# Spreading the work-ahead pieces of a rotor attention over twice as many steps between the experts

## The chip, the cores and the metric

One NeuronCore of a Trainium2 chip runs the whole program; the others are idle. The metric is device time in microseconds (us) from launch to end of one execution; the median of several runs is given. The engines are PE (matrix multiply, results to PSUM), DVE (vector), ACT (scalar and table functions), POOL (general vector work without access to PSUM) and SP (issues DMAs). Each engine works off its own instructions in the order in which they were written.

## The reference

Two transformer layers on x of shape (16, 256, 128), all in float32. Layer 0 is a 16-head attention and a mixture of 16 experts (the best 4 of each token, computed here for all experts and weighted with zeros). Layer 1 is a "rotor" attention and a gated feed-forward part. The change touches the expert part and the piece of layer 1's attention that runs beside it:

```python
# layer 0, experts
gu = jnp.einsum('th,ehf->tef', x, gate_up_proj) + gate_up_bias
gate = jnp.minimum(gu[..., ::2], LIMIT)
up = jnp.clip(gu[..., 1::2], -LIMIT, LIMIT)
act = (up + 1.0) * gate * jax.nn.sigmoid(gate * ALPHA)
out = jnp.einsum('te,teh->th', scores, jnp.einsum('tei,eih->teh', act, down_proj) + down_bias)
...
# layer 1, attention
k = jnp.exp(1j * (k_real * PHASE_SCALE))
rotors = jnp.exp(1j * (t[:, None, None] * freqs))[None]
out_pos = holo(v, rotors, jnp.conj(rotors))        # real(cumsum(v * binder) * probe) / sqrt(t)
out_assoc = holo(v, jnp.conj(k_shifted), k)
out = (out_pos * g_pos + out_assoc * g_assoc).reshape(Bb, Tt, HD) @ Wo
```

A "piece" below is one of eight products of this kind for one block of 128 of the 1024 columns: position or association (`pos`, `assoc`), batch element k of two, cosine or sine s. Each takes a product with the binder, a running sum along time, a product with probe and gate, and an addition to a total.

## The kernel before

The batch is cut into eight chunks of two elements (512 tokens). The program has three stages: layer 0's attention, the experts, and layer 1.

The expert stage is a loop over 128 steps (`n`, lines 1044 to 1082): step n is expert e = n % 16 of chunk c = n // 16. Each step issues PE's matmuls of gate and up into PSUM (`gate_up`, line 759), their evacuation (DVE `g`, line 767; ACT `u`, line 769; ACT's Silu, line 772; POOL's clip, line 773), for the step before, DVE's product (line 779) and POOL's product with the routing weight (line 780) (`act`), and the down matmul of three steps before (`down`, line 783). `pg` has three PSUM buffers and `pup` two. The engines' order is the order of writing (`manual_schedule`), so where a piece of other work is written within a step is where it stands in every queue.

Other work is laid between these steps: 

- The chunk before is ended at e = 2 (`chunk_end1`); at e = 3 `into_stream` (line 800) transposes it on PE into the one-buffer PSUM pool `p_m` and DVE adds it to `x`; at e = 5 `figures` takes mean and variance, at e = 7 POOL's `normalizer` follows, and the next chunk's routing weights are transposed (`spread_scores`).
- `prepare` (line 813) is a generator called once a step: layer 1's modulation, the rotor angles (`angles`), scaled weights, and last `first_steps` (line 942), the first two projections of layer 1 with their sines and binders.
- `part_ahead` (line 876), also called once a step, computes for one chunk the last of the eight column blocks of layer 1's attention (j = 7) and keeps the sum in `totals`. It starts at e = 10 of the next chunk (e = 8 in the last): normalized tokens, transposes, projections `pv` and `pk`, `off` (ACT rounds, then DVE subtracts), sines and cosines, and the eight pieces: POOL `bind`, DVE `read` (a scan, a product, an addition) one step later. In every chunk but the last one piece a step; in the last two.
- `last_end` (line 1018) ends the last chunk's layer-0 attention and works off its routing on DVE, up to about chunk 2.

`p_m` has one buffer, so each user of it waits until the one before is read out. `past_others` (line 937) lets `first_steps` stay clear of steps that use it. `turn_rotor` (line 990) turns a block of angles into cosines and sines on ACT: blocks 7 and 6 in `prepare`, the others in the sine step of `part_ahead`.

The third stage (from line 1085) runs 57 steps of layer 1, with two long scans a step on DVE, three products on POOL and ten or more matmuls on PE.

Of the kernel before, what the change touches and what calls it, by code (L numbers as in the profile page):

```python
# [11 lines left out]
F32 = mybir.dt.float32  # L12
AF = mybir.ActivationFunctionType
ALU = mybir.AluOpType
# [4 lines left out]
P = 128  # L19
B, T, D = 16, 256, 128  # L20
NIT = T // P
NCH = B // 2
# [12 lines left out]
NE, TOPK = 16, 4  # L35
# [19 lines left out]
def tile_adaln_two_layers(ctx: ExitStack, tc: tile.TileContext, a: dict, out: bass.AP):  # L55
    nc = tc.nc
# [23 lines left out]
    half_pi = const.tile([P, 1], F32, tag="half_pi", name="half_pi")  # L80
# [47 lines left out]
    gates = const.tile([P, NJ, 2], F32, tag="gates", name="gates")  # L128
# [98 lines left out]
    with ExitStack() as moe_scope:  # L227
# [64 lines left out]
        cross = moe_scope.enter_context(tc.tile_pool(name="cross", bufs=2))  # L292
# [21 lines left out]
        with ExitStack() as scope:  # L314
# [5 lines left out]
            p_m = scope.enter_context(tc.tile_pool(name="pa_m", bufs=8, space=bass.MemoryType.PSUM))  # L320
# [368 lines left out]
            for n in range(len(rounds) + LAG + 1):  # L689
                if n < len(rounds):  # L690
# [4 lines left out]
                    s = scores(n)  # L695
# [41 lines left out]
        w_k1 = load_late("w_k1", [P, HD], a["Wk"])  # L737
# [4 lines left out]
        with ExitStack() as scope:  # L742
# [12 lines left out]
            keep_all, row = sums[:, 0, 0:1].to_broadcast([P, T]), sums[:, 1, :]  # L755
# [57 lines left out]
            def prepare():  # L813
# [62 lines left out]
            def part_ahead(c):  # L876


                j = NJ - 1
                tokens(c)  # L880
                yield
                yield
                into_tokens(c, turned(c, hns.pop(c), p_m, "a1"))
                yield
                flat = hTs[c].rearrange("p k t -> p (k t)")
                v = cross.tile([P, 2, T], F32, tag="o", name=f"v_ahead_{c}")
                pv = p_m.tile([P, 2, T], F32, tag="m", name=f"pv0_{c}")
                nc.tensor.matmul(pv, w_v1[:, ts(j, P)], flat, start=True, stop=True)
                nc.scalar.copy(v, pv)
                bound = {}  # L890

                def bind(nm, k, s, by):
                    t = cross.tile([P, T], F32, tag=("heads", "y")[s], name=f"bound_ahead_{nm}_{c}_{k}_{s}")
                    nc.gpsimd.tensor_tensor(t, v[:, k, :], by, ALU.mult)
                    bound[nm, k, s] = t

                def read(nm, k, s, i, probe):
                    dst = totals[c][:, k, :]
                    nc.vector.tensor_tensor_scan(row, keep_all, bound.pop((nm, k, s)), 0.0, ALU.mult, ALU.add)  # L899
                    first = i == 0 and s == 0  # L900
                    nc.vector.scalar_tensor_tensor(
                        dst if first else row, row, gates[:, j, i : i + 1], probe, ALU.mult, ALU.mult
                    )
                    if not first:
                        nc.vector.tensor_tensor(dst, row, dst, ALU.add)
# [3 lines left out]
                pieces = [  # L909
                    ("pos", k, s, 0, rotor[:, j, s, :], rotor[:, j, s, :]) for k in range(2) for s in range(2)  # L910
                ] + [("assoc", k, s, 1, cs[:, s, k, 0:T], cs[:, s, k, 1:]) for k in range(2) for s in range(2)]
                many = 2 if c == AHEAD - 1 else 1

                def go(i):
                    for q in pieces[max(i - 1, 0) * many : i * many]:
                        read(*q[:4], q[5])
                    for q in pieces[i * many : (i + 1) * many]:
                        bind(*q[:3], q[4])

                for i in range(8 // many + 1):  # L920
                    yield
                    if i == 0:
                        pk = p_m.tile([P, 2, T], F32, tag="m", name=f"pk0_{c}")
                        nc.tensor.matmul(pk, w_k1[:, ts(j, P)], flat, start=True, stop=True)
                        off = cross.tile([P, 2, T], F32, tag="hn4", name=f"off_ahead_{c}")
                        nc.scalar.activation(off, pk, AF.Copy, bias=ROUND)
                        nc.vector.scalar_tensor_tensor(off, off, ROUND, pk, ALU.subtract, ALU.subtract)
                    if i == 1:
                        nc.scalar.activation(cs[:, 1, :, 1:], off, AF.Sin, scale=-TWO_PI_IN)
                        nc.scalar.activation(off, off, AF.Abs)  # L930
                        nc.scalar.activation(cs[:, 0, :, 1:], off, AF.Sin, bias=half_pi, scale=-TWO_PI_IN)

                        for r in {2: (0,), 3: (1,), 4: (2,), 5: (3,), 6: (4, 5)}.get(c, ()):
                            turn_rotor(r)
                    go(i)

            def past_others():

                while at["step"] % NE in (3, 7):
                    yield  # L940

            def first_steps():

                flat = hTs[0].rearrange("p k t -> p (k t)")
                for n in range(2):
# [6 lines left out]
                    nc.scalar.copy(v, pv)  # L952
                    firsts[n] = {"v": v}
                    yield
                    yield from past_others()
# [4 lines left out]
                    off = whole  # L960
                    nc.vector.scalar_tensor_tensor(off, whole, ROUND, pk, ALU.subtract, ALU.subtract)
                    cs = phasor[n]
                    yield
# [23 lines left out]
                hTs[c] = hT2[c]  # L987
                modulated(c, pt, 0, 1, [hTs[c][:, k, :] for k in range(2)])

            def turn_rotor(j):  # L990

                cos, sin = rotor[:, j, 0, :], rotor[:, j, 1, :]
                nc.scalar.activation(cos, sin, AF.Abs)
                nc.scalar.activation(cos, cos, AF.Sin, bias=half_pi, scale=-1.0)
                nc.scalar.activation(sin, sin, AF.Sin)

            both = [P, 2, 2, T]
            firsts = {}
# [44 lines left out]
            at, ahead = {}, []  # L1043
            for n in range(total + 4):
# [508 lines left out]
```

## Time and profile before

| | us |
|---|---|
| median of three runs | 1106.1 (1105.72 to 1106.27) |
| the profiled execution | 1105.43 |
| its span, first to last instruction | 1103.6 |
| expert stage, first gate matmul | 302.6 |
| expert stage, last down matmul's end | 702.4 |

In the profile each engine's busy time is given as a share of the span; "idle before" is the time in which an engine had nothing running before an instruction, with the instruction whose end released it. The costliest groups that belong to the expert stage are these; columns are line, engine, operation, out<-in with shapes and count, then busy us and mean ns of one, then idle us before them and what ended most of it:

```profile
L780 POOL TENSOR_TENSOR u<-u,wide 128x512 f32<-128x512 f32 x128 | 164.0, 1281 | 37.0 <-DVE u L779 29.2
L788 PE MATMUL acc<-u,w_dn 128*128 128x512 f32 x256 | 133.4, 603 | 9.8 <-POOL u L780 9.7
L763 PE MATMUL pg<-hT,w_gu 128*128 128x512 f32 x256 | 133.0, 601 | 8.3 <-DVE u L779 7.8
L765 PE MATMUL pup<-hT,w_gu 128*128 128x512 f32 x256 | 130.8, 592 | 0.0
L767 DVE TENSOR_SCALAR g<-pg,b_gu 128x512 f32<-128x512 f32 x128 | 95.4, 745 | 41.0 <-PE pg L763 39.8
L779 DVE SCALAR_TENSOR_TENSOR u<-u,pg 128x512 f32<-128x512 f32 x128 | 86.9, 679 | 24.4 <-POOL u L773 23.3
```

Each matmul of 512 columns is two instructions, whose ends the profile models; successive starts are closer than the mean length.

### The profile page before, as it was taken

To read this page: it belongs to the slowest core of one execution; us is meant where nothing else is said; L and a number is where in the kernel's file an instruction comes from. 1 tells how busy PE (TensorE), PEld (TensorE's weight loads), DVE (VectorE), ACT (ScalarE), POOL (GpSimd) and SP (SyncE) were. 2 spreads that over 40 slices of the span, in tenths; PEclk is the share of its full clock that TensorE was granted. 3 is DMA by queue.
4 is the path that set the end of the run, shared out by engine and by line. 5 is a ranking of instruction groups with operands and counts; after the bars stand their busy time and mean duration, and the time that the engine had idled before them with its cause. 6 is when DMAs were issued, how large, how long until landed. Compare 5 with 4: busy or idle time off the path is not lost.

```text
span 1103.6 us, 16066 instructions
## 1 busy us (share of the span) xinstructions
PE 1028.1 (93%) x5319; PEld 516.5 (47%) x5319; DVE 911.4 (83%) x1417; ACT 689.5 (62%) x1391; POOL 803.6 (73%) x762
## 2 busy tenths in 40 slices
PE   7999999999999999999899999797999999999987
PEld 5566666666644444444344444233343443434333
DVE  6678878998565886978486877998999999999994
ACT  3676667666656465566666465464666657667573
POOL 3335443552567677777679877799999999999992
PEclk9999999999999999999999999899999999999999
DMA  3102100000142222222222222000000000000000
GB/s 115 41 15 65 51 2 3 3 4 2 63 148 79 80 94 97 77 96 79 77 78 96 81 92 76 1 0 1 1 0 10 0 11 10 1 10 1 10 6 24
DMA packets 31955, 46.80 MB, mean 42 GB/s; under 512 B 8032, under 2 KB 22784, under 8 KB 31872
## 3 DMA queue, kind: packets, MB, share of 16 engines
q1 hardware_dynamic: 31328, 45.51, 12.3%
q8 instruction: 42, 0.69, 0.2%
q14 instruction: 41, 0.34, 0.1%
q10 hardware_dynamic: 544, 0.26, 0.1%
HBM read 43.13 MB, written 2.37 MB: 41 GB/s over the span
## 4 chain that ended last, share of the span: by engine, by line
PE 49%; DVE 28%; ACT 9%; POOL 6%; issue 6%; DMA 1%; SPq 0%; DVEq 0%; ACTq 0%; POOLq 0%
DVE sum_assoc L1153 6%; DVE mem L1153 6%; PE acc L788 5%; PE pg L763 5%; PE s L403 5%; PE pup L765 5%; PE st L437 5%; PE po L457 5%; PE pout L1167 4%; DVE m_pos L1384 4%; POOL u L780 2%; DVE sums L899 2%; DVE u L779 2%; PE pq L530 2%; DVE g L767 1%
## 5 line engine op out<-in xcount | busy, mean ns | idle before, releaser
L780 POOL TENSOR_TENSOR u<-u,wide 128x512 f32<-128x512 f32 x128 | 164.0, 1281 | 37.0 <-DVE u L779 29.2
L445 ACT ACTIVATE exp<-st 128x512 f32<-128x512 f32 x256 | 132.2, 602 | 85.9 <-PE st L437 85.9
L415 DVE TENSOR_REDUCE maxima<-s 128x2 f32<-128x512 f32 x256 | 158.9, 684 | 26.3 <-PE s L403 26.0
L1167 PE MATMUL pout<-m_pos,w_pos 128*128 128x512 f32 x228 | 114.8, 627 | 30.8 <-DVE m_pos L1384 20.8
L788 PE MATMUL acc<-u,w_dn 128*128 128x512 f32 x256 | 133.4, 603 | 9.8 <-POOL u L780 9.7
L763 PE MATMUL pg<-hT,w_gu 128*128 128x512 f32 x256 | 133.0, 601 | 8.3 <-DVE u L779 7.8
L769 ACT ACTIVATE u<-pup,b_gu 128x512 f32<-128x512 f32 x128 | 87.0, 680 | 74.3 <-PE pup L765 69.4
L1153 DVE TENSOR_TENSOR_SCAN sum_assoc<-keep,bound_assoc 128x1024 f32<-128x1024 bf16 x57 | 129.9, 2279 | 2.0 <-POOL bound_assoc L1150 1.9
L765 PE MATMUL pup<-hT,w_gu 128*128 128x512 f32 x256 | 130.8, 592 | 0.0
L1153 DVE TENSOR_TENSOR_SCAN mem<-keep,bound_pos 128x1024 f32<-128x1024 bf16 x57 | 129.5, 2272 | 0.0
L767 DVE TENSOR_SCALAR g<-pg,b_gu 128x512 f32<-128x512 f32 x128 | 95.4, 745 | 41.0 <-PE pg L763 39.8
L1150 POOL TENSOR_TENSOR bound_assoc<-v,phasor 128x1024 f32<-128x1024 f32 x56 | 122.1, 2181 | 4.5 <-ACT phasor L1140 4.5
L1389 POOL TENSOR_TENSOR sum_assoc<-sum_assoc,phasor 128x1024 f32<-128x1024 f32 x57 | 124.5, 2184 | 0.7 <-DVE sum_assoc L1153 0.7
L1150 POOL TENSOR_TENSOR bound_pos<-v,rotor 128x1024 f32<-128x1024 f32 x56 | 122.4, 2185 | 1.9 <-DVE sums L899 1.9
L773 POOL TENSOR_SCALAR u<-u 128x512 f32<-128x512 f32 x128 | 81.4, 636 | 57.9 <-ACT u L769 50.9
L772 ACT ACTIVATE pg<-g 128x512 f32<-128x512 f32 x128 | 76.2, 595 | 67.2 <-DVE g L767 66.9
L1167 PE MATMUL pout<-sum_assoc,w_assoc 128*128 128x512 f32 x228 | 107.5, 594 | 0.0
L779 DVE SCALAR_TENSOR_TENSOR u<-u,pg 128x512 f32<-128x512 f32 x128 | 86.9, 679 | 24.4 <-POOL u L773 23.3
L1117 ACT ACTIVATE whole<-pk 128x512 f32<-128x512 f32 x55 | 32.8, 596 | 87.9 <-PE pk L1116 86.4
L1167 PEld LDWEIGHTS pout<-m_pos,w_pos 128*128 128x128 f32 x228 | 40.6, 193 | 100.5 <-DVE m_pos L1384 50.3
L788 PEld LDWEIGHTS acc<-u,w_dn 128*128 128x128 f32 x256 | 46.8, 190 | 77.5 <-issue 38.5
L437 PE MATMUL st<-qx,kx 32*128 32x256 f32 x1024 | 81.8, 387 | 1.0 <-DMA qx<-turned 0.9
(300 smaller groups left out, 1878.3 us busy)
## 6 DMA issues: line engine op xcount, KB each, us to landing
wide<-scores SPq DMA_DIRECT2D x64, 512.0 KB
qx<-turned SPq DMA_DIRECT2D x256, 1.0 KB
w_gu<-in_gate_up_dram SPq DMA_DIRECT2D x8, 256.0 KB
out_dram<-x SPq DMA_DIRECT2D x16, 128.0 KB
x<-in_x_dram SPq DMA_DIRECT2D x14, 128.0 KB
w_dn<-in_down_dram SPq DMA_DIRECT2D x4, 256.0 KB
ga<-ga_rows SPq DMA_DIRECT2D x1, 768.0 KB
w_k<-in_Wk_dram SPq DMA_DIRECT2D x1, 512.0 KB
```

Of the source, the lines that this page charges most:

```text
L415: nc.vector.tensor_reduce(mx[:, :, g], s[g], AX.X, ALU.max, negate=True)
L437: nc.tensor.matmul(st[g][:, i, :], ks[c][rows_, r // NS, k, ts(i, P)], qs[c][r][rows_, k, :], start=True, stop=True,)
L445: nc.scalar.activation(e[:, g, :, :], st[g], AF.Exp, scale=QSCALE)
L763: nc.tensor.matmul(pg, w_gu[:, e, 0 : 2 * D : 2], h2, start=True, stop=True)
L765: nc.tensor.matmul(pu, w_gu[:, e, 1 : 2 * D : 2], h2, start=True, stop=True)
L779: nc.vector.scalar_tensor_tensor(u, u, 1.0, pg, ALU.add, ALU.mult)
L780: nc.gpsimd.tensor_tensor(u, u, wide[n // SOME][:, n % SOME, :], ALU.mult)
L788: nc.tensor.matmul(accs[c], w_dn[:, e, :], work.pop(n), start=False, stop=(e == NE - 1))
L1150: nc.gpsimd.tensor_tensor(w[nm], v2, bind, ALU.mult)
L1153: nc.vector.tensor_tensor_scan(dst.rearrange("p s k t -> p (s k t)"), keep.rearrange("p s t -> p (s t)"), work[n][nm].rearrange("p s k t - ...
L1167: nc.tensor.matmul(pos[c], w[:, j, :], m[:, k, :, :].rearrange("p k t -> p (k t)"), start=(j == 0 and i == 0 and k == 0), stop=(j == PARTS ...
L1389: nc.gpsimd.tensor_tensor(m, m, phasor[(n - 1) % 3][:, :, :, 1:], ALU.mult)
```

## The change

`part_ahead` now binds and reads a piece every second step, with the association pieces first, and the addition to the total (`added`) a step after the read; for the last but one part the addition comes at once, and the last part keeps its two pieces a step. The sine and the cosine are one step each (in the last part in one step), from a second tile `size`; DVE's `off` is taken in the step after PE's product `pk`, and so is `off` of `first_steps`. `into_stream` is split: transposes at e = 3, DVE's addition at e = 4. `prepare` takes the angles from step 38 on instead of 44, and turns rotor blocks 0 to 5 itself, two steps each, after the scaled weights. `past_others` also keeps clear of e = 10 to 15, and for two steps where the bank is held that long.

```diff
-            def into_stream(c, o):
+            def with_tokens(c, o):
                 pt = p_m.tile([P, 2, NIT, D], F32, tag="m", name=f"pmo_{c}")
                 for k in range(2):
                     for i in range(NIT):
                         nc.tensor.transpose(pt[:, k, i, :], o[:, k, ts(i, P)], ident)
+                return pt
+
+            def into_stream(c, pt):
                 for k in range(2):
                     b = 2 * c + k
                     nc.vector.tensor_tensor(x[b], pt[:, k], x[b], ALU.add)
...
-                while at["step"] < 44:
+                while at["step"] < 38:
                     yield
                 for p in range(NJ // 2 - 1):
                     yield from angles(p)
...
                         nc.scalar.activation(w[:, j, :], w_assoc[:, j, :], AF.Copy, scale=gates[:, j, i : i + 1])
+                    yield
+                for j in range(NJ - 2):
+                    turn_rotor(j, (0,))
+                    yield
+                    turn_rotor(j, (1, 2))
                     yield
...
+                written = set()
+
                 def read(nm, k, s, i, probe):
-                    dst = totals[c][:, k, :]
                     nc.vector.tensor_tensor_scan(row, keep_all, bound.pop((nm, k, s)), 0.0, ALU.mult, ALU.add)
-                    first = i == 0 and s == 0
-                    nc.vector.scalar_tensor_tensor(
-                        dst if first else row, row, gates[:, j, i : i + 1], probe, ALU.mult, ALU.mult
-                    )
-                    if not first:
+                    dst = row if k in written else totals[c][:, k, :]
+                    nc.vector.scalar_tensor_tensor(dst, row, gates[:, j, i : i + 1], probe, ALU.mult, ALU.mult)
+
+                def added(k):
+                    if k in written:
+                        dst = totals[c][:, k, :]
                         nc.vector.tensor_tensor(dst, row, dst, ALU.add)
+                    written.add(k)
...
+                nc.scalar.activation(off, pk, AF.Copy, bias=ROUND)
+                if c == AHEAD - 1:
+                    for q in pos_[0:2]:
                         bind(*q[:3], q[4])
...
+                yield
+                nc.vector.scalar_tensor_tensor(off, off, ROUND, pk, ALU.subtract, ALU.subtract)
+                nc.scalar.activation(size, off, AF.Abs)
+                nc.scalar.activation(cs[:, 1, :, 1:], off, AF.Sin, scale=-TWO_PI_IN)
+                if c < AHEAD - 1:
+                    yield
+                nc.scalar.activation(cs[:, 0, :, 1:], size, AF.Sin, bias=half_pi, scale=-TWO_PI_IN)
+                if c == AHEAD - 1:
+
+                    pieces = pos_ + assoc_
+                    for i in range(4):
+                        for q in pieces[2 * i : 2 * i + 2]:
+                            read(*q[:4], q[5])
+                            added(q[1])
+                        for q in pieces[2 * i + 2 : 2 * i + 4]:
+                            bind(*q[:3], q[4])
+                        yield
+                else:
+                    pieces = assoc_ + pos_
+                    for i in range(9):
+                        if i:
+                            yield
+                            q = pieces[i - 1]
+                            read(*q[:4], q[5])
+                            if c == AHEAD - 2:
+                                added(q[1])
+                        if i < 8:
+                            q = pieces[i]
+                            bind(*q[:3], q[4])
+                        yield
+                        if i and c < AHEAD - 2:
+                            added(pieces[i - 1][1])
+
+            def past_others(steps=1):
+
+                while any((at["step"] + i) % NE in (3, 7, *range(10, 16)) for i in range(steps)):
                     yield
...
                 if e == 3 and 1 <= c < NCH:
-                    into_stream(c - 1, o)
+                    pt = with_tokens(c - 1, o)
+                if e == 4 and 1 <= c < NCH:
+                    into_stream(c - 1, pt)
```

More of the change, by code (lines that the diff above doesn't have):

```diff
@@ L908, in part_ahead @@
                 nc.gpsimd.memset(cs[:, :, :, 0:1], 0.0)
[L909 to L917, printed above, removed]
-                        bind(*q[:3], q[4])
@@ L920, in part_ahead @@
-                for i in range(8 // many + 1):
-                    yield
[L922 to L935, printed above, removed]
@@ L937, in past_others @@
-            def past_others():
-                while at["step"] % NE in (3, 7):
+                pos_ = [("pos", k, s, 0, rotor[:, j, s, :], rotor[:, j, s, :]) for k in range(2) for s in range(2)]
+                assoc_ = [("assoc", k, s, 1, cs[:, s, k, 0:T], cs[:, s, k, 1:]) for k in range(2) for s in range(2)]
+                yield
+                pk = p_m.tile([P, 2, T], F32, tag="m", name=f"pk0_{c}")
+                nc.tensor.matmul(pk, w_k1[:, ts(j, P)], flat, start=True, stop=True)
+                off, size = (
+                    cross.tile([P, 2, T], F32, tag="hn4", name=f"{nm}_ahead_{c}") for nm in ("off", "size")
+                )
@@ L954, in first_steps @@
                     yield
-                    yield from past_others()
+                    yield from past_others(2)
                     pk = p_m.tile([P, 2, T], F32, tag="m", name=f"pk1_{n}")
@@ L960, in first_steps @@
                     off = whole
+                    yield
                     nc.vector.scalar_tensor_tensor(off, whole, ROUND, pk, ALU.subtract, ALU.subtract)
@@ L988, in into_tokens, with turn_rotor @@
                 modulated(c, pt, 0, 1, [hTs[c][:, k, :] for k in range(2)])
-            def turn_rotor(j):
+            def turn_rotor(j, which=(0, 1, 2)):
                 cos, sin = rotor[:, j, 0, :], rotor[:, j, 1, :]
-                nc.scalar.activation(cos, sin, AF.Abs)
-                nc.scalar.activation(cos, cos, AF.Sin, bias=half_pi, scale=-1.0)
-                nc.scalar.activation(sin, sin, AF.Sin)
+                if 0 in which:
+                    nc.scalar.activation(cos, sin, AF.Abs)
+                if 1 in which:
+                    nc.scalar.activation(cos, cos, AF.Sin, bias=half_pi, scale=-1.0)
+                if 2 in which:
+                    nc.scalar.activation(sin, sin, AF.Sin)
             both = [P, 2, 2, T]
```

## The prediction

> **What bounds the kernel now.** I read the whole span by engine first, then stretches of it. The expert part is 128 steps, one expert of one chunk each, from 302.6 us to about 702 us of the span. The windows view, cut at the starts of chunks 0 to 7 (columns: from:to and length, then busy time and count of PE, weight loads, DVE, ACT, POOL, then granted clock, DMA share, GB/s), says:
>
> ```profile
> PE 1028.1 (93%) x5319; PEld 516.5 (47%) x5319; DVE 911.4 (83%) x1417; ACT 689.5 (62%) x1391; POOL 803.6 (73%) x762
> 347.90:396.60 48.70, 47.19 (x124) 21.31 (x123) 38.02 (x68) 26.86 (x50) 34.58 (x39) 1.00 0.25 89
> 396.60:446.10 49.50, 47.16 (x115) 20.19 (x114) 37.79 (x72) 32.03 (x55) 37.61 (x45) 1.00 0.24 86
> 446.10:495.20 49.10, 46.35 (x116) 20.43 (x115) 40.99 (x75) 30.58 (x58) 39.26 (x45) 1.00 0.26 86
> 495.20:547.90 52.70, 48.85 (x120) 21.04 (x119) 36.21 (x67) 33.91 (x71) 37.41 (x48) 1.00 0.26 90
> 547.90:597.60 49.70, 48.33 (x120) 21.11 (x119) 36.17 (x67) 31.36 (x59) 40.36 (x49) 1.00 0.22 75
> 597.60:645.10 47.50, 46.30 (x116) 20.51 (x115) 35.15 (x66) 27.35 (x51) 38.21 (x47) 1.00 0.25 91
> 690.00:706.70 16.70, 9.24 (x17) 3.27 (x15) 16.10 (x29) 6.38 (x14) 10.62 (x15) 0.87 0.00 0
> ```
>
> PE is busy nearly throughout, yet chunks that do the same work take 47.5 to 49.5 us. A step with nothing extra takes 2.57 us from one gate matmul to the next. Step 3 takes 1.26 us more (bias matmul), each set of four transposes 0.43 (steps 3, 7, 12), each extra projection 0.86 (steps 13, 14). So an undisturbed chunk is 16 x 2.575 + 1.26 + 3 x 0.43 + 2 x 0.86 = 45.5 us. What lies above it is stall. The timeline of chunk 6, steps 7 to 10, shows the two kinds (start, length, engine, line, tile, idle before and its releaser); the PE wait table for the whole stretch follows.
>
> ```profile
> 616.80 0.18 DVE L183 BATCH_NORM_AGGREGATE mv_a<-stats_a 128x2 f32<-128x6 f32 x1
> ...
> 619.31 0.42 DVE L905 TENSOR_TENSOR total<-sums,total 128x256 f32<-128x256 f32 x1
> 619.65 0.74 DVE L767 TENSOR_SCALAR g<-pg,b_gu 128x512 f32<-128x512 f32 x1
> 620.31 0.68 DVE L779 SCALAR_TENSOR_TENSOR u<-u,pg 128x512 f32<-128x512 f32 x1
> 620.90 0.69 DVE L899 TENSOR_TENSOR_SCAN sums<-sums,und_ahead_assoc 128x256 f32<-128x256 f32 x1
> 621.63 0.49 DVE L901 SCALAR_TENSOR_TENSOR sums<-sums,gates,phasor_ahead 128x256 f32<-128x256 f32 x1
> 622.15 0.42 DVE L905 TENSOR_TENSOR total<-sums,total 128x256 f32<-128x256 f32 x1
> ```
> ```profile
> PE pg L763 <- DVE u L779: 7.8, 9, 1.4
> PE acc L788 <- POOL u L780: 6.5, 9, 0.9
> PE pk L924 <- DVE whole L961: 1.4, 1, 1.4
> PE pv L888 <- ACT v L952: 0.7, 1, 0.7
> ```
>
> **First kind:** from step 15 to step 6 DVE reads one piece a step; at step 5 four rows' figures come on top, and PE's gate matmul of step 8 finds no free bank until DVE's product of step 5 is done. **Second kind:** PE has then waited for DVE, and POOL, following DVE, reaches the normalizer of step 7 (0.23 + 1.04 + 0.20 + 0.20, some 1.8 us with gaps) so late that the product of step 7 is not there when PE wants it in step 10. The last stretch, 690 to 706.7, is bound by DVE alone: 16.1 busy of 16.7.
>
> **The change, part by part.** Prices on DVE are from start to start in the timeline, since the ends overlap the next start: gate 0.66, product 0.59, scan 0.72, probe 0.53, add 0.34; so a read is 1.25 and, with its add, 1.59. POOL: clip 0.61, product 1.27, a piece's binder 0.69.
>
> *Pieces every other step.* Nothing is removed; eight reads and six adds a chunk go from steps 15 to 6 to even (read) and odd (add) steps over the whole chunk. An even step now holds 1.25 + 1.25 = 2.5 us of DVE, an odd one 1.59, PE's step being 2.57. The heaviest pair is step 4 (the stream's addition, 0.67, moved here: 3.2) and step 5 (figures 1.6, add 0.34: 3.2): DVE falls 1.2 us behind, and recovers by step 7 (1.25 against 3.0). PE tolerates about 2.7 us (DVE's gate follows PE's by 1.06, then 0.66 + 0.68, so its product ends 2.4 us into a step and is wanted two steps, 5.15 us, after that step's start). So the first kind should go. For POOL I walk on from step 3's start, with whole lengths to be safe: DVE's product 6 ends at 16.3, POOL's 6 at 17.7, the normalizer at 19.5, clip 8 at 20.1, product 7 at 21.45; PE wants it at 21.86 (steps 3 to 9 last 4.26, 3 x 2.57, 3.0, 2 x 2.57, then two matmul pairs of 0.86). So the second kind goes too, with 0.4 us to spare. The stalls by chunk (length less 45.5, less 0.86 for each first-layer projection in it: two in chunks 4 and 5; less 0.9 for chunk 1's router matmuls and gap), and what I expect to remain:
> - chunk 1: 2.4. DVE also works off the routing, one operation group a step, and waits 2.06 us at step 3 for the transposes. With the addition moved to step 4, three routing operations (1.5 us) fill this hole. 0.9 stays.
> - chunk 2: 4.0, of which 1.8 at steps 1 to 3 come from ACT, which loads tables for the routing's exponential, then a sine, then the Silu (below). The first sine now stands behind DVE's `off` a step later, which I put at 0.6 us more: 2.4 stays.
> - chunk 3: 3.6. The rotor angles (two DVE operations of 0.87 at steps 5 and 6) still meet the figures: about 1.3 stays.
> - chunk 4: 5.5, with the two waits on the single `p_m` bank (1.4 and 0.7) that the new rule on steps 10 to 15 excludes: 0 stays.
> - chunk 5: 2.5. The first-layer projection now falls on step 4, where the bank waits for the delayed addition: DVE ends it 3.3 us into the step, PE asks at 2.57. 0.75 stays.
> - chunk 6: 2.0. First-layer binders (1.18 on POOL) land at steps 7, 9, 11; with 0.4 us to spare, 1.5 stays.
> - chunk 7 up to step 14: 2.0, nothing stays.
>
> Sum: 22.0 before, 6.9 after, 15.1 us gained.
>
> *PE's last product taken a step later.* DVE waits 12.8 us in all for `off` (7 times) and 2.1 once for the transposes. Apart from the places counted above this is idle time of an engine with 1.3 to 2.0 us of work in that step: nothing more. What it adds: `p_m` is held a step longer; the next user is four steps away except in chunk 5.
>
> *Sines one operation a step; rotors moved into preparation.* ACT's total is the same; preparation starts six steps earlier (no DMA among what moves) and gains twelve steps, each at most 0.91 us of ACT where ACT has 1.28 of work. In the last chunk 2.6 us of ACT leave step 13. Cover: ACT's free half of each step; if it were gone, the next `u` and clip would come 0.9 us late, and still be inside the tolerance. The whole run loads tables five times, the last at 402.9 us (1.28 each); after that sines and Silus alternate in five chunks without a load. So I take 0 for it.
> The Trainium skill's "ScalarE: Activation LUTs", Table sets: the hidden batching unit, speaks against it: batch calls by set, since each switch is a load (about 2.7 us there, 1.28 for the load alone in this trace). The rule counts sets, not functions; by the trace one set holds both here, so it gives 0; were it two, the rival below would come.
>
> *The tail.* The part of chunk 5 now lasts to step 128 and meets that of chunk 6, where DVE is the bound: two of its reads with adds (steps 126 and 128, 2 x 1.59) and `off` (0.6, from a free step into a full one) join the queue that ends in the second layer's first products: +3.8 us. DVE is 367 us busy of the following 397, so this is not won back.
>
> Bounds: the middle can give 0 (all stalls keep) to 18 (only chunk 2's 2.4 and the angles stay); the tail can cost 0 (if other waits hide it) to 17 (below). I take 15.1 and 3.8, as each is nearest to steps the trace shows without a stall, and to a DVE stretch without a gap.
>
> Sum against the profiled run (1105.4 us: span 1103.6, the rest around it): 1105.4 - 15.1 + 3.8 = 1094.1; the median of the runs is 0.7 above the profiled one: **1095 us**, its own range 1090 to 1099.
>
> **Rivals.**
> 1. *POOL becomes the bound.* Steps 6 to 10 hold 2.57, 3.7, 2.57, 1.9, 2.57 = 13.3 us of POOL against 13.3 of PE, so any lateness at step 6 keeps the 0.9 us stall of step 10. For: the spare 0.4. Against: POOL had 1.77 us idle there waiting for DVE. Six chunks x 0.9 = 5.4 kept: 1100.
> 2. *The tail eats it (slower).* The parts of chunks 5 and 6 share two binder buffers each of `heads` and `y`; with both running, POOL's next binder must wait for DVE to read the other part's, with clip and product queued behind it, and DVE's product waits for the clip. If each of steps 125 to 128 runs serially, POOL's 0.69 x 2 + 0.61 + 1.27 = 3.2 is added four times: 13 + 3.8 = 17 against 15.1: 1108. It decides from a tail of 15 us on. For: the buffers do interleave. Against: DVE's own queue there, 4.6 to 5.8 us a step, covers 3.2.
> 3. *The change does little:* the stalls stay, moved by a step, and pay for the tail: 1104 to 1108.
> 4. *Table switches:* each of the twelve added sine steps costs two loads of 1.28: at most 31 us, 1126 with none hidden. Against: the five loads above.
>
> **Chances.** Forecast 0.55; rival 1 0.20; rival 2 0.10; rival 3 0.12; rival 4 0.03. A difference under 0.2% (2.2 us) cannot be told from none. Faster: 0.55 + 0.20 + 0.03 (of rival 3) = 0.78; same 0.07; slower 0.15. The range 1089 to 1107 takes in the forecast, rival 1 and most of rival 3.
>
> **What would show it.** PE's waits for DVE's product (7.8) under 2.5 us in the stretch to 690, those for POOL's product (6.5) under 3; chunk 4 some 5 us shorter, chunk 7 up to step 14 some 2; the stretch from step 13 of chunk 7 to the second layer's first transposes longer by about 4. It is wrong if POOL's product still ends PE's wait at step 10 of each chunk, if DVE idles in the tail for POOL's clip, or if table loads stand between sines.

## The result: 1094.3 us, and the profile after

| | before | after |
|---|---|---|
| median of the runs, us | 1105.91 (1105.20 to 1106.27) | 1094.31 (1092.60 to 1095.53) |
| the profiled execution, us | 1105.43 | 1095.53 |
| its span, us | 1103.6 | 1093.7 |
| first gate matmul to chunk 7, step 14 ("middle") | 384.82 | 368.27 |
| from there to the second layer's first transposes ("tail") | 19.33 | 23.12 |

The changed kernel takes 0.9895 times as long, with a 95% interval of 0.9878 to 0.9912. The windows view of the changed kernel, cut at the starts of chunks 1 to 7, at step 14 of chunk 7, and at the tail's end, has the columns from:to and length, then busy time and count of PE, weight loads, DVE, ACT and POOL, then granted clock, DMA share and GB/s:

```profile
349.56:397.57 48.01, 47.11 (x125) 21.35 (x124) 39.00 (x68) 26.84 (x51) 34.33 (x38) 1.00 0.26 90
397.57:445.21 47.64, 46.12 (x116) 20.53 (x115) 37.82 (x71) 33.63 (x60) 38.09 (x45) 1.00 0.25 90
445.21:491.13 45.92, 45.84 (x116) 20.53 (x115) 37.79 (x72) 32.28 (x66) 37.49 (x45) 1.00 0.27 92
491.13:536.63 45.50, 45.50 (x116) 20.70 (x115) 34.81 (x66) 33.35 (x70) 37.09 (x46) 1.00 0.27 94
536.63:584.57 47.94, 47.46 (x120) 21.38 (x119) 35.61 (x67) 29.14 (x55) 37.17 (x48) 1.00 0.26 88
584.57:632.66 48.09, 47.83 (x120) 21.23 (x119) 35.05 (x66) 28.97 (x53) 39.92 (x48) 1.00 0.25 88
632.66:672.55 39.89, 39.89 (x99) 18.08 (x98) 31.64 (x61) 23.06 (x43) 34.72 (x44) 1.00 0.26 93
672.55:695.67 23.12, 12.31 (x24) 4.24 (x22) 22.01 (x39) 6.55 (x13) 14.32 (x19) 0.74 0.00 0
```

PE is busy for the whole of chunk 4 (45.50 of 45.50) and of chunk 7 up to step 14 (39.89 of 39.89): there the stalls are gone. Chunks 5 and 6 hold the two first-layer projections each (1.72 us) that chunks 4 and 5 held before. The last row is the price: 23.12 us in which DVE is busy for 22.01.

The table of PE's waits for the same middle (columns: PE's instruction, what it waited for, us in total, times, longest) answers to the one shown of before:

```profile
PE acc L788 <- POOL u L780: 2.7, 4, 0.9
PE pg L763 <- DVE u L779: 1.1, 1, 1.1
PE pup L765 <- ACT u L769: 0.5, 1, 0.5
PE pv L978 <- DVE x L810: 0.5, 1, 0.5
PE pg L763 <- DVE logits L637: 0.4, 1, 0.4
```

The wait for DVE's product falls from 7.8 to 1.1, that for POOL's product from 6.5 to 2.7 (chunk 0, in which nothing was changed, holds 1.1 and 0.7 of these before and after, so that in the other chunks no wait for DVE's product is left), and the two waits on the single `p_m` bank (1.4 and 0.7) become one of 0.5 (`pv`, for the delayed addition). Rows from the timelines of DVE and POOL in steps 7 to 10 of chunk 6, two of the changed kernel and one of the kernel before (start, length, engine, line, operation, tile, and in brackets the idle time before it and its releaser):

```profile
610.07 0.75 DVE L767 TENSOR_SCALAR g<-pg,b_gu 128x512 f32<-128x512 f32 x1 [0.82 <-PE pg L763]
...
610.92 0.23 POOL L188 TENSOR_SCALAR rstd_a<-mv_a 128x4 f32<-128x4 f32 x1
```
```profile
625.16 0.23 POOL L188 TENSOR_SCALAR rstd_a<-mv_a 128x4 f32<-128x4 f32 x1
```

Before, DVE ran without a pause from step 7 to the start of step 10, and PE waited for it. Now it is DVE that waits for PE (0.82 before a gate at 610.07), and POOL's normalizer begins 4.93 us after step 7 does (610.92 less 605.99, where its gate matmul starts); before the change it was 7.87 us (625.16 less 617.29).

The difference of the two spans divides so: middle -16.55, tail +3.79, first layer's attention +1.69, rest of the second layer +1.17; together -9.90, and 1103.6 - 9.9 = 1093.7. The last two are not the change's. Over the profiles below the attention took 302.6 to 304.8 us and the second layer's rest 396.7 to 398.6, with the work there the same (397.18 in the kernel with more POOL work, whose third stage is the changed kernel's, against 398.03), while a chunk whose instructions stayed as they were repeats to 0.03 us. So the experiments are read by chunks, and the whole runs are given beside them.

### The profile page after: what moved, and what is told of

Its sections match the earlier page's. It is cut to its first block, busy times and chain, and to the rows that moved or that the text cites. A ratio compares the mean times of both kernels' runs of the same rounds, so it can differ in the third digit from the quotient of the medians.

```text
span 1093.7 us, 16044 instructions
## 1 busy us (share of the span) xinstructions
PE 1025.8 (94%) x5319; PEld 519.1 (47%) x5319; DVE 909.7 (83%) x1417; ACT 687.8 (63%) x1391; POOL 801.9 (73%) x762
## 4 chain that ended last, share of the span: by engine, by line
PE 58%; DVE 21%; ACT 8%; POOL 6%; issue 5%; DMA 1%; SPq 0%; DVEq 0%; ACTq 0%; POOLq 0%
PE pg L763 8%; PE acc L788 8%; PE pup L765 7%; PE s L403 6%; DVE sum_assoc L1187 5%; DVE mem L1187 5%; PE st L437 5%; PE po L457 5%; PE pout L1201 5%; DVE m_pos L1418 3%; PE pq L530 2%; POOL u L780 1%; PE pk L1150 1%; PE pk L538 1%; DVE maxima L415 1%
## 5 line engine op out<-in xcount | busy, mean ns | idle before, releaser
L767 DVE TENSOR_SCALAR g<-pg,b_gu 128x512 f32<-128x512 f32 x128 | 95.5, 746 | 60.5 <-PE pg L763 58.6
L772 ACT ACTIVATE pg<-g 128x512 f32<-128x512 f32 x128 | 76.1, 595 | 23.0 <-DVE g L767 22.6
```

Source lines behind the costliest of these rows:

```text
L767: nc.vector.tensor_scalar(g, pg, b_gu[:, 0, e : e + 1], LIMIT, ALU.add, ALU.min)
```

## The experiments

Lengths in us; a chunk runs from its first gate matmul to that of the next. Chunk 0, which takes 45.3 us in every kernel, is in the middle but not shown. Each row is one profiled execution.

| kernel | c1 | c2 | c3 | c4 | c5 | c6 | c7 to 14 | middle | tail |
|---|---|---|---|---|---|---|---|---|---|
| before | 48.73 | 49.51 | 49.07 | 52.68 | 49.70 | 47.50 | 42.33 | 384.82 | 19.33 |
| changed | 48.01 | 47.64 | 45.92 | 45.50 | 47.94 | 48.09 | 39.91 | 368.27 | 23.12 |
| new pace alone | 48.72 | 47.13 | 45.94 | 50.18 | 48.40 | 45.55 | 39.91 | 371.12 | 22.90 |
| all but the pace | 48.03 | 50.37 | 49.17 | 46.42 | 47.93 | 49.36 | 41.25 | 377.82 | 19.56 |
| the same, sines together | 48.03 | 50.50 | 49.20 | 47.94 | 48.70 | 49.35 | 42.06 | 381.07 | 19.56 |
| products in the same step | 48.72 | 46.37 | 45.95 | 45.50 | 47.22 | 48.03 | 39.91 | 366.98 | 22.91 |
| sines together | 48.02 | 49.81 | 45.94 | 45.56 | 47.93 | 48.12 | 40.00 | 370.68 | 23.13 |
| more POOL work | 48.01 | 47.64 | 45.92 | 45.50 | 48.06 | 48.09 | 41.63 | 370.12 | 23.12 |
| early end | 48.02 | 47.64 | 45.95 | 45.50 | 47.94 | 48.11 | 40.21 | 368.67 | 20.26 |
| mended | 48.02 | 47.00 | 45.94 | 45.50 | 47.22 | 47.21 | 40.22 | 366.39 | 20.26 |
| mended, last part tighter | 48.02 | 46.99 | 45.94 | 45.50 | 47.22 | 47.22 | 40.43 | 366.60 | 19.07 |

### The new pace alone

The kernel before, with only the pieces (their order, one every second step, the addition a step later) of the change:

```diff
-                for i in range(8 // many + 1):
-                    yield
...
-                    go(i)
+                    pieces = assoc_ + pos_
+                    for i in range(9):
+                        if i:
+                            yield
+                            q = pieces[i - 1]
+                            scanned(*q[:4], q[5])
+                            if c == AHEAD - 2:
+                                added(q[1])
+                        if i < 8:
+                            q = pieces[i]
+                            bind(*q[:3], q[4])
+                        yield
+                        if i and c < AHEAD - 2:
+                            added(pieces[i - 1][1])
```

`scanned` is `read` without its addition; the last part keeps two pieces a step.

> The kernel before with only the new pace and order of the pieces (read every second step, addition a step later, parts of the last two chunks as in the change); sines, rotors, `off`, stream addition and bank rule as before. Theory A (the pace spreads DVE's load and removes PE's stalls): from chunk 0's first gate matmul to chunk 7's step 14 it takes 370.0 us (before 384.8, changed kernel 368.3), chunk 4 keeps some 2.6 us of stall at steps 13 and 14, the stretch from step 14 to the second layer's first transposes grows by 3.2 us to 22.5; time 1094 to 1096. Theory B (the other parts free PE): the middle stays above 380 us, time 1104 or more.

It took 1097.03 us (1095.69 to 1100.17), ratio 0.9926 (0.9909 to 0.9944). The middle gains 13.70 of the change's 16.55, 1.1 less than theory A expected, and the tail grows by 3.57 of its 3.79. Chunks 3, 6 and 7 reach what the change gives or better. Chunk 4 stays at 50.18, since the two waits on `p_m` are as before (1.4 and 0.7 in this kernel's table of waits), and chunk 1 does not move at all: at its steps up to 10 no piece is read.

### All but the pace

The changed kernel with its pieces one a step again:

```diff
-                    for i in range(9):
-                        if i:
-                            yield
...
+                for i in range(2, 8 // many + 1):
+                    go(i)
+                    yield
```

> The change without the pace: one piece a step in the old order, all other parts as in the change (sines one a step, rotors in the preparation, `off` and the stream addition a step later, bank rule). Theory A: the middle takes 382 us (2.6 us of chunk 4 gained, 0.7 of chunk 1, 0.5 to 0.7 lost in chunk 5), the last stretch 19.9 us, time 1104. Theory B: the middle takes 372 us or less, time 1094 or less.

1100.38 us (1099.35 to 1102.72), ratio 0.9956 (0.9941 to 0.9970). The middle gains 7.00: 377.82, where 382 was expected. Besides the two waits on `p_m`, which are gone, chunk 4 has lost most of its stall for DVE's product, though its pieces come as they did before. The two halves alone give 13.70 + 7.00 = 20.7 against 16.55 together: 4.15 us, net, can be had from either half.

### All but the pace, with the sines together again

What lost chunk 4 its stall with the pace unchanged? This kernel also puts sine, cosine and the rotor blocks back into one step of the part, with as many steps in preparation as before:

```diff
+                nc.scalar.activation(cs[:, 0, :, 1:], size, AF.Sin, bias=half_pi, scale=-TWO_PI_IN)
+                for r in {2: (0,), 3: (1,), 4: (2,), 5: (3,), 6: (4, 5)}.get(c, ()):
+                    turn_rotor(r)
```

> The parts of the change other than the pace, but with the sines of a part and its rotor blocks again in one step. Theory C (the burst of up to six ACT operations at step 15 makes ACT, and so DVE, enter the next chunk late, and this lateness is the stall at step 7): chunks 4, 5 and 6, which were 46.4, 47.9 and 49.4 us with the rest alone, are 1.1 to 1.5 us longer each, and the stall stands at step 7 again. Theory D (the later takes on DVE removed it): these chunks stay within 0.2 us.

One run, 1103.42. Against the kernel above, chunk 4 grows by 1.52, chunk 5 by 0.77 and chunk 7 by 0.81; chunks 3 and 6 do not move. So theory C came for chunk 4 alone of the three it named: in chunk 5 the growth is PE's wait for the stream's addition (0.5 before, 1.2 here), and chunk 6's stall is one for POOL at step 10 in both kernels (4.68 and 4.67 us from this gate to the next). Four rows of this kernel's timeline, steps 1 to 8 of chunk 4, show how (ACT, POOL, DVE, PE):

```profile
500.92 0.67 ACT L769 ACTIVATE u<-pup,b_gu 128x512 f32<-128x512 f32 x1
...
501.68 0.61 POOL L773 TENSOR_SCALAR u<-u 128x512 f32<-128x512 f32 x1 [1.96 <-ACT u L769]
...
504.28 0.70 DVE L905 TENSOR_TENSOR_SCAN sums<-sums,bound_ahead_pos 128x256 f32<-128x256 f32 x1 [1.27 <-POOL bound_ahead_pos L899]
...
520.79 1.13 PE L763 MATMUL pg<-hT,w_gu 128*128 128x512 f32 x2 [0.96 <-DVE u L779]
```

From 498.12 to 501.02 ACT turns six sines and the like in a row, `u` behind them comes late (500.92), POOL idles 1.96 for it and binds the next piece late, and DVE idles 1.27 for that. DVE is then full, with a piece in each step, until the figures: these start 19.35 us after the chunk does (516.23 less 496.88), in the kernel above 17.83 (515.22 less 497.39). So the lateness that PE pays for at step 8 (520.79) was made six steps earlier, on ACT. With the new pace DVE has room to catch up and the same bunch costs chunk 4 no more than 0.06, as the next run shows.

### Sines together in the changed kernel

The same edit on the changed kernel, with the new pace.

> The changed kernel with the sines of a part and its rotor blocks again in one step. Theory C with the new pace: DVE has room to recover before step 7, so chunks 3 to 7 stay within 0.2 us of the changed kernel's (45.9, 45.5, 47.9, 48.1, 39.9) and only chunk 2 moves, by up to 0.7 us; the last stretch stays at 23.1 us, since DVE bounds it. If the sines pay also with the new pace, chunks 4 to 6 are 1 us longer each.

One run, 1096.1. Only chunk 2 moves, by 2.17 (47.64 to 49.81), where at most 0.7 was expected; no other chunk by more than 0.1. ACT's timeline at the start of chunk 2, first of the changed kernel, then of this one:

```profile
398.16 1.28 ACT L283 ACT_TABLE_LOAD   x1
...
401.08 0.63 ACT L934 ACTIVATE size_ahead<-off_ahead 128x512 f32<-128x512 f32 x1 [1.16 <-DVE off_ahead L933]
401.73 1.28 ACT L935 ACT_TABLE_LOAD   x1
403.03 0.63 ACT L935 ACTIVATE phasor_ahead<-off_ahead 128x512 f32<-128x512 f32 x1
...
404.25 1.28 ACT L772 ACT_TABLE_LOAD   x1
405.54 0.60 ACT L772 ACTIVATE pg<-g 128x512 f32<-128x512 f32 x1
406.08 0.71 ACT L938 ACTIVATE phasor_ahead<-size_ahead,half_pi 128x512 f32<-128x512 f32 x1
```
```profile
402.69 0.71 ACT L933 ACTIVATE phasor_ahead<-size_ahead,half_pi 128x512 f32<-128x512 f32 x1
403.30 0.67 ACT L769 ACTIVATE u<-pup,b_gu 128x512 f32<-128x512 f32 x1
403.99 1.28 ACT L772 ACT_TABLE_LOAD   x1
```

Within some seven microseconds ACT loads three tables: for the routing's exponential (L283), the sine, and the Silu (L772). There it has no free half of a step, and the cosine in front of `u` and Silu (402.69) makes both later by its own 0.6. The last load of the changed kernel stands before the Silu, and the cosine after it (406.08) runs without one.

That 0.6 is the smaller part of the 2.17. The rest is PE's own pace, as these rows show: PE after the wait in the changed kernel, then in this one, then a window of this kernel with the columns as above:

```profile
407.29 1.02 PE L763 MATMUL pg<-hT,w_gu 128*128 128x512 f32 x2
```
```profile
406.06 1.77 PE L788 MATMUL acc<-u,w_dn 128*128 128x512 f32 x2 [0.91 <-POOL u L780]
407.63 1.91 PE L763 MATMUL pg<-hT,w_gu 128*128 128x512 f32 x2
```
```profile
407.00:409.00 2.00, 2.00 (x3) 0.78 (x3) 1.87 (x4) 1.71 (x4) 1.83 (x3) 0.50 0.84 256
```

The granted clock is 0.50 here, while the changed kernel keeps 1.00 for the whole of chunk 2. From the start of this down matmul (406.06) to that of the bias matmul (L787, 410.53) PE needs 4.47 us, in the changed kernel 2.91 (406.33 to 409.24): 1.56 more, and 0.6 + 1.56 is the 2.17. In the kernel without the new pace the same bunch costs chunk 2 only 0.13 (50.37 to 50.50), with the clock at 1.00. One execution of this kernel was profiled, so that how often the clock falls there is not shown.

### The products taken in the same step again

The changed kernel, with `off` (twice) and the stream's addition back in the step of PE's product:

```diff
-                yield
                 nc.vector.scalar_tensor_tensor(off, off, ROUND, pk, ALU.subtract, ALU.subtract)
+                yield
...
-                    pt = with_tokens(c - 1, o)
-                if e == 4 and 1 <= c < NCH:
-                    into_stream(c - 1, pt)
+                    into_stream(c - 1, with_tokens(c - 1, o))
```

> The changed kernel with DVE's takes put back into the step of PE's product (stream addition at step 3, `off` of the parts and of the first projections at once). Theory A (these waits lay in DVE's idle time): against the changed kernel chunk 1 is 0.7 us longer, chunk 5 0.7 shorter, the last stretch 0.6 shorter, all else equal; time 1093 to 1095. Theory B (a DVE that waits for PE's last product stalls the next step): 0.5 to 1 us more in every chunk from 1 on; time 1099 or more.

1092.74 us (1090.92 to 1094.60), ratio 0.9881 (0.9863 to 0.9899): by the runs not told apart from the change, by the chunks 1.29 us shorter in the middle and 0.21 in the tail. The part of the change that took the products later so costs 1.5 us net. It gains 0.71 in chunk 1, where DVE had waited for the transposes at step 3, and loses 1.27 in chunk 2 and 0.72 in chunk 5. In chunk 2 the 1.27 lie between the gates of steps 2 and 3 (4.58 us in the changed kernel, 3.31 here), so ahead of the stream's addition, and the reason stands in the rows above: ACT waits 1.16 us for `off` (401.08), with the sine's table load, `u` and the Silu's load queued behind. In this kernel the same instruction has no wait:

```profile
400.38 0.61 ACT L934 ACTIVATE size_ahead<-off_ahead 128x512 f32<-128x512 f32 x1
```

DVE's waits show the trade: the changed kernel has none for `pmo`, this one 11.9 us in seven, but DVE's wait for PE's gate is 58.6 us in the changed kernel and 39.3 in this one. Idle time of DVE was moved, not won.

### More work on POOL

The changed kernel with 1, 2, 4 and 8 small products on POOL after the normalizer, at step 7 of chunks 2, 4, 5 and 7. Their results go nowhere.

```diff
+                    for i in range({2: 1, 4: 2, 5: 4, 7: 8}.get(c, 0)):
+                        nc.gpsimd.tensor_tensor(extra, neg_half4, neg_one, ALU.mult)
```

> The changed kernel with small products on POOL put behind the normalizer at step 7: one (0.3 us) in chunk 2, two (0.6) in chunk 4, four (1.2) in chunk 5, eight (2.3) in chunk 7. If POOL has 0.4 us to spare there, as predicted, the chunks grow by 0, 0.2, 0.8 and 1.9 us; if it has 1.1 us (counted by starts instead of whole lengths), by 0, 0, 0.1 and 1.2; if POOL is no limit there, by nothing. Chunks 3 and 6 stay as they are (45.9 and 48.1 us).

One run, 1094.76. In this kernel's timeline of POOL, chunk 7, and the PE matmul that is late by it:

```profile
657.61 2.14 POOL L1104 TENSOR_TENSOR extra<-neg_half,neg_one 128x4 f32<-128x4 f32 x8
...
660.53 1.27 POOL L780 TENSOR_TENSOR u<-u,wide 128x512 f32<-128x512 f32 x1
...
661.85 1.12 PE L788 MATMUL acc<-u,w_dn 128*128 128x512 f32 x2 [1.45 <-POOL u L780]
```

Eight take 2.14 us, 0.27 each. One and two of them cost nothing (47.64 and 45.50, to the hundredth), four (1.07 us) cost 0.12, eight cost 1.72. So POOL's spare there is some 1.0 us in chunk 5 and 0.4 to 0.5 in chunk 7, whose step 7 lacks the 0.43 us of transposes on PE.

### An early end for the part of chunk 5

The tail is put to the test: the reads of the last but one part go closer together from step 8 of chunk 7 on (the numbers in the code count the part's own calls), so that the last two come before step 14 of chunk 7.

```diff
+                elif c == AHEAD - 2:
+                    reads = {8: 0, 10: 1, 12: 2, 14: 3, 15: 4, 16: 5, 17: 6, 18: 7}
+                    binds = {6: 0, 8: 1, 10: 2, 12: 3, 14: 4, 15: 5, 16: 6, 17: 7}
```

> The changed kernel with the part of chunk 5 read faster from step 8 of chunk 7 on (steps 2, 4, 6, 8, 9, 10, 11, 12), so that none of its reads meets the last part's. If the tail's cost is DVE's extra work, two reads with additions at 1.59 us each, the last stretch falls from 23.1 to 19.9 us and chunk 7 up to step 14 stays within 0.5 us of 39.9; if POOL's wait for the shared binder buffers costs more than that, it falls below 19.3; time about 1091.

One run, 1092.75. The tail falls from 23.12 to 20.26, by 2.86, and chunk 7 grows by 0.30; all else is equal. DVE's busy time in the tail falls from 22.01 to 19.49, by 2.5: the tail was as long as DVE's queue, and two reads with their additions are most of what the change put into it.

### Mended

This early end, with four edits more: the first part begins at step 8, so that its sines keep clear of the routing's exponential; `off` of the parts is taken in PE's step; the first-layer projections keep clear of step 4; the first-layer binders on POOL keep clear of steps 6 to 10.

```diff
-                if e == (8 if c == AHEAD else 10) and 1 <= c <= AHEAD:
+                if e == (8 if c in (1, AHEAD) else 10) and 1 <= c <= AHEAD:
...
-                    yield from past_others()
+                    while at["step"] % NE in (3, 4, 7, *range(10, 16)):
+                        yield
...
+                        while at["step"] % NE in range(6, 11):
+                            yield
```

> The changed kernel with what the runs so far ask for: the last but one part read faster (as in early_end), DVE's `off` of a part again in the step of its product, the first part started two steps earlier (step 8 of chunk 1, so that its sines come before the routing's exponential), the first projections kept off step 4, and the first binders kept off steps 6 to 10. Chunk 2 falls from 47.6 to about 45.6 us, chunk 5 from 47.9 to 47.2, chunk 6 from 48.1 to 47.2, the middle from 368.3 to about 364.6, the last stretch from 23.1 to 19.4; time 1086 to 1088.

1088.37 us (1087.91 to 1092.31), ratio 0.9848 (0.9832 to 0.9865), below the change's interval. Chunk 5 gives 0.72, chunk 6 0.88 (PE is busy for 47.22 of 47.22 in each: no stall is left), the tail 2.86, where 3.7 was expected (`off` back in its step adds nothing to the early end), and chunk 2 0.64, where 2.0 was hoped for. Its loads are now two, but a stall stays, as ACT's timeline of this kernel shows:

```profile
398.51 1.28 ACT L283 ACT_TABLE_LOAD   x1
399.89 0.47 ACT L283 ACTIVATE rt_exp<-rt_exp 128x320 f32<-128x320 f32 x1
400.26 0.67 ACT L769 ACTIVATE u<-pup,b_gu 128x512 f32<-128x512 f32 x1
400.95 1.28 ACT L772 ACT_TABLE_LOAD   x1
...
406.12 0.60 ACT L772 ACTIVATE pg<-g 128x512 f32<-128x512 f32 x1 [2.66 <-DVE g L767]
```

ACT waits 2.66 us for DVE's gate. A part that starts two steps earlier also reads two steps earlier, and its first read now stands on DVE between the routing's last operations (402.52 to 404.3) and the gate (405.35).

### Mended, with the last part tighter

```diff
-                yield
+                if c < AHEAD - 1:
+                    yield
...
-                    reads = {8: 0, 10: 1, 12: 2, 14: 3, 15: 4, 16: 5, 17: 6, 18: 7}
+                    reads = {8: 0, 9: 1, 12: 2, 13: 3, 14: 4, 15: 5, 16: 6, 17: 7}
...
```

> The kernel of the run before (all mends), and two pieces of work moved a few steps forward: the last part starts one step tighter, so that its last additions end a step earlier, and the part of chunk 5 is read at steps 2, 3 and 6 to 11 of chunk 7's end instead of 2, 4, 6 and 8 to 12. Theory A (the tail is as long as the queue that DVE has left at step 14): one and a half reads less in the queue, tail from 20.3 to about 18.5 us, middle 366.4 give or take 0.5, chunk 7 to step 14 up to 0.5 us longer, time about 1086.5. Rival (DVE's total alone bounds the whole stretch from chunk 7's middle to the second layer, so that what leaves the tail comes back as stall before step 14): chunk 7 to step 14 and tail together fall by no more than 0.5 us, time 1088.

1089.70 us (1089.06 to 1090.80), ratio 0.9848 (0.9832 to 0.9864): not told apart from the kernel above. Tail and chunk 7 together fall by 0.98 us, between the two theories (1.8 and at most 0.5). DVE had 1.8 us less to do in the tail (17.65 against 19.49 busy), but the tail fell by only 1.19, since another chain now ends with it. In this kernel's timeline:

```profile
685.77 1.26 POOL L780 TENSOR_TENSOR u<-u,wide 128x512 f32<-128x512 f32 x1 [2.71 <-DVE u L779]
687.09 2.08 PE L788 MATMUL acc<-u,w_dn 128*128 128x512 f32 x2 [2.82 <-POOL u L780]
689.20 1.23 DVE L1436 TENSOR_TENSOR m_pos<-mem,rotor 128x1024 f32<-128x1024 f32 x1 [0.37 <-PE acc L788]
```

From DVE's last product on, POOL's product and the last down matmul follow in a row, and DVE waits for them (0.37), which it did nowhere in the tails before. What is left to gain in the tail is no longer only DVE's.

## Why the prediction was right, point by point

The forecast was 1095 us with a middle 15.1 shorter and a tail 3.8 longer; measured were 16.55 and 3.79, and 1094.3 in the median. The mechanism is the one named, but that the total fits to 0.7 us is partly luck. Middle and tail alone gained 12.8 where 11.3 stood; chunk 1 gave 0.8 less than its term, chunks 2, 3, 6 and 7 gave 0.3 to 0.9 more; and the stages that were not touched took 2.9 us more in the profiled execution.

- **The pace, and DVE's stalls (first kind).** Right. The waits for DVE's product fell below the 2.5 named, DVE waits for PE, and the new pace alone removes most of them. But it is not the only cure for all of them: in chunk 4 spreading the sines takes 1.52 of the same stall away where the pace is the old one. Pricing each part alone would have counted it twice.
- **POOL at step 10 (second kind).** The direction was right, the spare was mis-sized: 0.4 by whole lengths, 0.4 to 1.0 measured. So rival 1 did not come, and chunk 6 kept 0.87 of its stall instead of 1.5: of its first-layer binders some found room. The mended kernel, which moves them out of these steps and the projections out of step 4, keeps none.
- **Chunk 1.** The term that fell short by most: 0.72 gained where 1.5 stood. The moved addition does fill DVE's wait at step 3, and that is all the 0.72 (same-step kernel: 48.72). The other half was taken for the same stall, but it is POOL's. PE waits 0.79 at step 10 for a product that stands behind the normalizer on POOL, and the normalizer is late because POOL waits 1.68 us for DVE, which works off routing operations of 1.27 and 0.78 us there (timelines of POOL and DVE of the changed kernel). No piece is in these steps, so the pace can't cure it:

```profile
375.86 1.27 POOL L780 TENSOR_TENSOR u<-u,wide 128x512 f32<-128x512 f32 x1 [1.68 <-DVE u L779]
377.10 0.47 POOL L188 TENSOR_SCALAR rstd_a<-mv_a 128x4 f32<-128x4 f32 x1
```
```profile
372.43 1.27 DVE L268 TENSOR_TENSOR rt_at<-rt_left,rt_most 128x320 f32<-128x320 f32 x1
```

 The 1.27 goes with POOL's work beside it: the same routing product takes 0.54 at 381.32. It ends 0.35 us after POOL's product beside it does, here (373.70 after 373.35) as there (381.86 after 381.51), and so does the other product of 1.27 (L273 at 376.20: 377.47 after 377.13), as if DVE could finish it only when POOL was done. No run tests this.

- **Chunk 2.** 1.87 gained, 1.6 forecast; near in the sum, with two terms wrong. The later `off` costs 1.27, not 0.6; one sine a step gives 2.17, by the one run that puts the sines together, and had been put at nothing. ACT's free half of a step was the cover named for that zero, and among the three table loads this cover is not there; that is 0.6 of the 2.17. The other 1.56 is PE at half clock, for which the prediction had no term.
- **Chunks 3, 4, 5, 7.** 3.15, 5.46 (less the projections that moved out of it, 1.72), 1.76 (0.72 stays, 0.75 said) and 2.42, against 2.3, 5.5, 1.75 and 2.0. In chunk 3 the rotor angles were to keep 1.3 and keep 0.42, and do so with the new pace alone, too. In chunk 5 the cause named, the projection behind the delayed addition at step 4, is the one: with the addition back at step 3 it is 47.22.
- **Products a step later, priced at nothing beyond chunks 1, 2 and 5.** Right in what was left out, wrong in what it comes to: those three sum to a loss of 1.3 us, and 1.5 with the tail.
- **The tail.** 3.8 forecast, 3.79 measured; the new pace alone brings 3.57, all but the pace 0.23. The later `off` was put at 0.6 and cost 0.2, and the two reads were worth a little more than their 3.18: the fit to 0.01 is two misses that cancel.
- **Rival 2, the shared binder buffers.** Its mechanism is there, and its cover holds. In the changed kernel's tail POOL waits for DVE to read out a binder:

```profile
680.94 0.64 POOL L902 TENSOR_TENSOR und_ahead_assoc<-v_ahead,phasor_ahead 128x256 f32<-128x256 f32 x1 [1.05 <-DVE sums L908]
685.57 0.73 POOL L902 TENSOR_TENSOR und_ahead_assoc<-v_ahead,phasor_ahead 128x256 f32<-128x256 f32 x1 [0.54 <-DVE sums L908]
```

 DVE itself waits for nothing in that tail, so these 1.6 us cost nothing.
- **Rivals 3 and 4.** The whole interval of the ratio lies below 0.998, so that the stalls did not just move. And no table switches came: the changed kernel loads five tables in all, as before, and none after the Silu's load shown above. By the Trainium skill's "ScalarE: Activation LUTs", Table sets: the hidden batching unit, sets and not functions decide; the trace agrees, with a cosine at 406.08 after a Silu and no load. But it is not one set for all: the set loaded for the sine at 401.73 didn't serve the Silu, which loaded its own at 404.25, and that one serves both.

## What to carry to other kernels

Work laid between the steps of a matrix pipeline should be spread until no step of the vector engine holds more than PE's step, and then judged at the places where something else comes on top (a table load, a normalizer, routing): a price of "nothing, it is hidden" holds only where the cover is really free, so look for each instance by itself. Taking a product a step later fills the waiting engine's hole, but whatever stands behind that engine's result moves a step later too; here it cost more than it gave. Spreading also pushes the last instances past the end of the loop: what had been free there becomes tail, and the last instance deserves its own, tighter schedule.

## What the runs showed of the hardware

- The granted clock follows PE's idleness within a few microseconds. In the changed kernel's tail, windows of 4 us (columns as above) read, after two in which the clock was 1.00:

```profile
681.00:685.00 4.00, 0.91 (x2) 0.50 (x2) 3.79 (x8) 0.60 (x1) 3.01 (x4) 0.81 0.00 0
685.00:689.00 4.00, 2.10 (x3) 0.50 (x2) 3.85 (x10) 0.00 (x0) 2.02 (x3) 0.50 0.00 0
```

 After PE had been busy for 0.91 of 4 us, it was granted half speed, and the last down matmuls, two instructions, took 2.08 us instead of 1.12 (the kernel before, at the same place). The Trainium skill's "TensorE: Matmul & The Clock Gate", Part 1: The HAM clock gate, says that the clock is half or full and is taken back after a window of idleness. The two values agree (0.81 and 0.70 are means of windows in which it changed), but PE need not have been idle throughout: before the fall in chunk 2 of the kernel with the sines together it had no pause longer than 1.16 us. There windows of 1 us from 405 to 411 read 1.00, 0.70, 0.50, 0.50, 0.59 and 1.00, so that half speed lasted some 3.4 us and cost the 1.56 told above. A stretch bound by DVE so makes PE slow just where its chain ends, which is what the last experiment met.
- A chunk of 46 us whose work is the same repeats to 0.03 us between kernels and on two chips (chunk 3: 45.92 to 45.95), while the stages before and after it scatter by 1 to 2 us. A gain of half a microsecond that the whole runs can't show is plain when the same stretch is compared.
